# Image 0's keys and values as products of quarters, and the weight sums of p and z moved one image on

## The chip, the cores and the metric

The kernel runs on one core of a Trainium2 chip. The metric is the device time of one execution in microseconds (us). Before the change the median of three runs is 2768.2 us (2767.59 to 2768.71).

## What is computed

The input has B = 8 images of C = 512 channels and T = 32 x 32 = 1024 positions, in float32. Two attention blocks follow each other, each with a residual. The reference, cut to what matters:

```python
def _L0_conv_ref(x, ...):                       # 8 heads of 64 channels
    h = group_norm(x)                           # 32 groups
    qkv = einsum('oc,bct->bot', w_qkv, h) + b_qkv
    weight = softmax(einsum('bct,bcs->bts', q * scale, k * scale))
    a = einsum('bts,bcs->bct', weight, v)
    return x + einsum('oc,bct->bot', w_proj, a) + b_proj

def _L1_conv_ref(x, ...):                       # one head of 512 channels
    xn = group_norm(x)                          # 8 groups
    q, k, v = (conv1x1(xn, w, b) for each)
    attn = softmax(einsum('bqc,bck->bqk', q, k) * C**-0.5)
    out = einsum('bqk,bkc->bqc', attn, v)
    return x + conv1x1(out, p_w, p_b)
```

## The kernel before

**Names.** q, k, v and p are the weights of the first block (p its output projection). The second block's four weights are folded into two products of weights, made once: m (keys with queries) and z (output projection with values). A tile of 128 partitions holds 128 channels, so an image is four tiles of 128x1024. A "big" tile is one of a pool of `NBIG` equal buffers; `wpool` holds three buffers for weights.

**Products by halves.** A product of a 512x512 weight with an image is not made with eight products of halves but with seven (the Strassen-Winograd scheme). `left_sums` makes the sums of weight blocks, `right_sums` those of image blocks, and `wino` (line 229) orders the seven products over three PSUM banks a, b and c. That is "halves once". `conv` makes a product by channel (queries and keys), `by_token` (line 379) makes values, where positions lie on the partitions.

`conv2` (line 536) goes by halves twice: each of the seven products is split again into seven, so 49 products of quarters. It needs two further sets of sums:

- the inner factors of the image (`inner_factors`, line 423): 7 times 4 subtractions of 128x256 on GpSimd (POOL);
- the second sums of the weight (`keep2_steps`, line 302): after the four first sums of 128x512 on VectorE (DVE), four sums of 128x896, then seven stores to DRAM (`wdram2`). `load_weight` (line 340) brings them back, one part at a time, in the order of the list `uses` (line 333).

In `conv2`, ScalarE copies and DVE additions empty PSUM, and POOL adds a few finished blocks to others (`more`). The last two steps of each stretch are put on the list `tail` and are run by `finish` after the first product of the next stretch.

**Order of the work.** Matmuls stand in TensorE's queue in the order of the program (`keep_in_program_order`), and so do many operations of the other engines. `prologue` (line 936) does, in this order: transposes of two weights of the second block (`natural`, line 893), the product m (`product`, line 903) with the group norm of image 0 in between, then for image 0 the values, queries and keys, all by halves once; then transposes of a third weight (tr_wv), the mean of image 1's group norm, the bias products, the product z (ps_wz, 32 matmuls) and the variance of image 1's group norm. DVE makes v's second sums, POOL those of q, k, m and p. Stores and loads are issued by SyncE (SP), in order too.

**Attention of the first block.** `attention0` (line 677) goes over four pairs of heads (hp) and two halves of the queries (tb), so eight tiles, here numbered 0 to 7: tile n is hp n // 2, tb n % 2. In a tile TensorE makes scores sc (8 pieces), ScalarE their exponentials e, DVE adds the e's up in `total` (seven additions of 128x1024: one of line 698, six of line 700), and TensorE then makes av from the e's and v. After each second tile (tb = 1) `reciprocals` (line 631) has TensorE sum `total` over partitions (`sums`); these matmuls stand in TensorE's queue ahead of the next tile's sc, and wait for DVE's last addition of the tile just done. Then DVE copies `line`, SP sends it through DRAM (rows, cols, all_rows, r; DVE makes recs from cols on the way), and a tile later DVE multiplies a by r.

Other work is hung into 16 slots of this loop: slot 2n stands before av of tile n, slot 2n + 1 after it. An operation in a slot stands in its engine's queue at that place of the program. In image 0 slot 3 holds z's first sums (DVE), slots 5, 7, 9 and 11 one of z's second sums each (POOL), slot 12 their stores and two loads. Image 1's slots 4 and 5 hold mean and variance of the second block's group norm.

```python
for f in extra.pop(0) if extra else ():      # attention0: slot 2n
    f()
av = acc_tile(f"av_{uid}")
...
after = extra.pop(0) if extra else []        # slot 2n + 1
```

## Time and profile before

| What | Value |
|---|---|
| median of three runs | 2768.2 us |
| profiled execution | 2768.3 us, span 2765.8 us |
| mean granted TensorE clock | 0.999 |
| TensorE busy | 2753.6 us of the span |
| VectorE, ScalarE, GpSimd busy | 2045.6, 998.4, 1291.4 us |
| first attention of image 0 begins | 117.85 us |
| image 0: v, then q, then k | from 25.25, from 49.50, to 97.56 us |

The page gives each engine's busy time, and the chain of work that ended last, followed back from the last instruction. The view of waits lists what an engine waited for. A timeline gives an engine's instructions from the start of the span, equal neighbours in one line: start, duration of all, engine, line, operation, output<-input, shapes, count, and in brackets the idle time before with what ended it. Matmuls are pipelined, so a step's length on TensorE is read from start to start.

### The profile page before, as it was taken

What the parts mean: (1) busy time and instruction counts of PE and PEld (TensorE: products, weight loads), DVE (VectorE), ACT (ScalarE), POOL (GpSimd) and SP (SyncE); (2) the same over time, 40 slices, a digit from 0 to 9 for tenths busy, and PEclk for the clock granted to TensorE, in tenths of its full rate; (3) what the DMA queues carried; (4) which work ended last, traced back from release to release, by engine and by line L of the source; (5) the groups of instructions that cost most, each with busy time, mean ns of one, the idle gap of its engine ahead of it and who ended that gap; (6) DMA issues with size and microseconds to landing.
All of it is one profiled execution on the core that took longest, in us unless ns stands there. A gap on an engine that the chain in (4) does not pass through costs nothing.

```text
span 2765.8 us, 36809 instructions
## 1 busy us (share of the span) xinstructions
PE 2753.6 (100%) x13436; PEld 1762.1 (64%) x13436; DVE 2045.6 (74%) x3214; ACT 998.4 (36%) x1307; POOL 1291.4 (47%) x1384
## 2 busy tenths in 40 slices
PE   9999999999999999999999999999999999999999
PEld 5437736776376853868538694486844968348585
DVE  6587777777777777777777867777678776787776
ACT  1253454214632146312453125531255313633130
POOL 2313605745067440774307752176621766146763
PEclk9999999999999999999999999999999999999999
DMA  7827412344113441144401443114521145112302
GB/s 265 253 91 252 181 32 70 138 159 166 40 63 138 170 162 32 63 161 167 150 24 63 177 182 119 32 55 184 196 98 49 58 153 216 59 54 97 142 24 74
DMA packets 126070, 332.60 MB, mean 120 GB/s; under 512 B 19831, under 2 KB 64695, under 8 KB 114362
## 3 DMA queue, kind: packets, MB, share of 16 engines
q1 hardware_dynamic: 125294, 329.75, 33.6%
q8 instruction: 108, 1.77, 0.3%
q14 instruction: 80, 0.66, 0.1%
q10 hardware_dynamic: 588, 0.42, 0.1%
HBM read 258.14 MB, written 71.99 MB: 119 GB/s over the span
## 4 chain that ended last, share of the span: by engine, by line
PE 99%; DVE 1%; DMA 0%; issue 0%; SPq 0%; DVEq 0%
PE sc L60 16%; PE av L60 16%; PE psb_av L60 6%; PE psb L60 5%; PE psa_av L60 4%; PE psc_av L60 4%; PE psc L60 4%; PE psa L60 3%; PE psb_v L60 3%; PE psb_k L60 3%; PE psb_p L60 3%; PE psb_q L60 3%; PE psb_g L60 3%; PE psb_z L60 3%; PE psc_z L60 2%; PE psa_k L60 2%
## 5 line engine op out<-in xcount | busy, mean ns | idle before, releaser
L700 DVE TENSOR_TENSOR sum<-sum,e 128x1024 f32<-128x1024 f32 x384 | 473.9, 1234 | 35.5 <-ACT e L696 0.9
L696 ACT ACTIVATE e<-sc 128x1024 f32<-128x1024 f32 x512 | 476.1, 1053 | 63.1 <-PE sc L60 62.6
L60 PE MATMUL sc<-q,k 64*128 64x512 f32 x2048 | 456.8, 596 | 0.0
L60 PE MATMUL av<-e,v 128*64 128x512 f32 x2048 | 453.4, 595 | 0.0
L60 PEld LDWEIGHTS sc<-q,k 64*128 64x128 f32 x2048 | 190.1, 185 | 245.9 <-ACT e L696 120.9
L60 PEld LDWEIGHTS av<-e,v 128*64 128x64 f32 x2048 | 141.4, 137 | 299.0 <-issue 288.2
L434 POOL TENSOR_TENSOR inner_h<-x 128x256 f32<-128x256 f32 x16 | 14.8, 924 | 415.9 <-DVE x L1028 415.9
L698 DVE TENSOR_TENSOR sum<-e,e 128x1024 f32<-128x1024 f32 x64 | 79.9, 1249 | 103.6 <-ACT e L696 103.6
L719 ACT COPY a<-av 128x512 f32<-128x512 f32 x64 | 37.5, 586 | 320.1 <-PE av L60 280.6
L126 POOL TENSOR_TENSOR rstd<-ve,mhalf 128x4 f32<-128x4 f32 x16 | 18.8, 1177 | 274.0 <-DVE ve L124 274.0
L60 PE MATMUL psb<-inner,inner_h 128*128 128x256 f32 x448 | 115.6, 380 | 0.0
L60 PE MATMUL psa_av<-e,z 128*128 128x512 f32 x256 | 112.5, 592 | 0.0
L482 ACT COPY psb_v<-psa_v 128x512 f32<-128x512 f32 (+1 forms) x28 | 14.5, 517 | 232.5 <-DVE x L845 176.6
L60 PEld LDWEIGHTS psb<-inner,inner_h 128*128 128x128 f32 x448 | 84.5, 190 | 13.6 <-POOL inner L449 2.1
L60 PE MATMUL psb_z<-w_z,inner_h 128*128 128x128 f32 x672 | 87.5, 276 | 0.0
L60 PE MATMUL psb_g<-inner_h,w_m 128*128 128x256 f32 x336 | 84.9, 381 | 0.0
L776 ACT ACTIVATE e<-e 128x1024 f32<-128x1024 f32 x64 | 65.1, 1052 | 46.7 <-DVE e L766 25.6
L60 PEld LDWEIGHTS psb_z<-w_z,inner_h 128*128 128x128 f32 x672 | 81.4, 192 | 0.5
L60 PEld LDWEIGHTS psa_av<-e,z 128*128 128x128 f32 x256 | 47.4, 190 | 53.6 <-issue 51.7
L771 POOL TENSOR_TENSOR e<-e,e 128x512 f32<-128x512 f32 x64 | 79.3, 1271 | 2.0 <-DVE e L766 1.8
L571 POOL TENSOR_TENSOR v<-v,v 128x256 f32<-128x256 f32 x28 | 20.1, 726 | 125.3 <-DVE u_v L566 121.3
L820 POOL TENSOR_TENSOR t<-e,t 128x1024 f32<-128x1024 f32 x32 | 78.4, 2482 | 0.0
(443 smaller groups left out, 6138.0 us busy)
## 6 DMA issues: line engine op xcount, KB each, us to landing
r<-all_rows SPq DMA_DIRECT2D x78, 256.0 KB
x<-in_x SPq DMA_DIRECT2D x36, 512.0 KB
h<-in_x SPq DMA_DIRECT2D x32, 512.0 KB
spill<-x SPq DMA_DIRECT2D x32, 512.0 KB
x<-spill SPq DMA_DIRECT2D x32, 512.0 KB
out<-x SPq DMA_DIRECT2D x63, 256.0 KB
kept<-a SPq DMA_DIRECT2D x28, 512.0 KB
again<-kept SPq DMA_DIRECT2D x28, 512.0 KB
```

The lines of the kernel that those rows point to most:

```text
L60: tc.keep_in_program_order(nc.tensor.matmul(*args, **kw))
L126: nc.gpsimd.tensor_tensor(rstd, ve, mhalf, ALU.pow)
L434: pin(engine.tensor_tensor(dst, x, y, ALU.subtract))
L482: nc.scalar.copy(ps["b"], ps["a"])
L571: nc.gpsimd.tensor_tensor(d, x, y, ALU.add)
L696: nc.scalar.activation(e, sc, AF.Exp, scale=(C // 8) ** -0.5)
L698: nc.vector.tensor_add(total, es[0], e)
L700: nc.vector.tensor_add(total, total, e)
L719: nc.scalar.copy(dst, av)
L771: nc.gpsimd.tensor_tensor(blocks(dst, r, cc)[0], blocks(x, r, cc)[0], blocks(y, r, cc)[0], ALU.add)
L776: nc.scalar.activation(e[c, cc, r], e[c, cc, r], AF.Exp, scale=scale)
L820: on = lambda *a: lambda: tc.keep_in_program_order(nc.gpsimd.tensor_tensor(*a))
```

## The change

Of image 0, only the queries still go by halves once, and they come first. Keys and values go through `conv2`. Their second sums are made in place of the weight tile and used straight from there (`own`), with no loads. The order of the new prologue: m with the norm of image 0, q, transposes tr_wv, bias products (in bank c), three quarters of z's product, k (with z's last quarter, deferred into `tail`, behind k's first products), v. DVE makes k's second sums, POOL the inner factors and the second sums of v, q and m. `natural` copies wq in two halves. Image 1's mean and variance move into slots 0 and 1 of image 0's attention, in two halves of 64 columns.

p's sums, and the store of its first sums (`keep`, 1.8 MB), move from the prologue to the slots of image 0's attention that z's held. z's move to image 1's attention: loads at the start of that iteration, first sums in slot 5 (DVE), second sums in slots 6 and 7 (POOL), stores and two loads in slot 12; `uses` is shifted to suit.

```diff
-NBIG = 34
+NBIG = 35
...
-        def keep2_steps(n, t, engine=nc.gpsimd, pin=lambda ins: ins):
-
-            if engine is nc.gpsimd:
-                u = wpool.tile([P, 4, 7, P], F32, tag="w", name=f"prepare2_{n}")
-                u = [u[:, i, :, :] for i in range(4)]
-            else:
-                u = [big_tile(f"prepare2_{n}_{i}", (P, 7, P)) for i in range(4)]
+        def second_sums(n, t, engine, pin=lambda ins: ins, inside=True):
+
             quarter = lambda k, i: t[:, :, k, ts(i, P)]
             a11, a21, a12, a22 = quarter(0, 0), quarter(0, 1), quarter(1, 0), quarter(1, 1)
-            s1, s2, s3, s4 = u
+            if inside:
+                s3 = a21
+                s1, s2, s4 = (big_tile(f"prepare2_{n}_{i}", (P, 7, P)) for i in range(3))
+            else:
+                u = wpool.tile([P, 4, 7, P], F32, tag="w", name=f"prepare2_{n}")
+                s1, s2, s3, s4 = (u[:, i, :, :] for i in range(4))
+            f2 = (a11, a12, s4, a22, s1, s2, s3)
...
         for b in range(1, B - 1):
-            uses += [*twice["m"], *twice["z"], *layer0, *twice["p"]]
+            m0, m1 = twice["m"]
+            uses += [m0, *([None] * 2 * (b == 1)), m1, *twice["z"], *layer0, *twice["p"]]
...
+        def z_factors():
+            t, steps = prepare("z")
+            sums = second_sums("z", t, nc.gpsimd, pin, False)[1]
+            load = lambda: load_weight(pin)
+            return {5: steps, 6: sums[:2], 7: sums[2:4], 12: [sums[4], load, load]}
...
-        def natural(wt, nm, banks):
+        def natural(wt, nm, banks, cut=1):
...
-            spread(lambda o, copy: tc.keep_in_program_order(copy(t[o], pt[o])), KC)
+            for h in range(cut):
+                spread(lambda o, copy: tc.keep_in_program_order(copy(t[o][:, ts(h, C // cut)], pt[o][:, ts(h, C // cut)])), KC)
...
+            for ic in range(KC - defer):
+                part(ic)
+            if defer:
+                tail.append(lambda: part(KC - 1))
...
-            for f in first["v"][1]:
+            for f in first["q"][1]:
                 f()
-            background.extend(steps)
-            background.extend(first["q"][1])
-            v = by_token(weight_factors(first["v"][0]), hf, "v0_0", middle=(2, 5, 6, 7), back=4)
+            inner, ih = inner_factors(hf, "h0_0", tc.keep_in_program_order)
+            background.extend([*steps, *first["k"][1], ih[6], *ih[:6]])
+            q = conv(weight_factors(first["q"][0]), hf, pcols("bq0"), "q0_0", middle=(2, 5, 6, 7), back=4)
             finish()
-            run_background(len(background))
-            keep2("v", first["v"][0], nc.vector)
-            background.extend(first["k"][1])
-            x1 = [load_x(1, c, "x1") for c in range(KC)] if B > 1 else []
-            norm1 = GroupNorm(0, "0_1")
-            background.extend(lambda c=c: norm1.stats(c, x1[c]) for c in range(len(x1)))
-            q = conv(weight_factors(first["q"][0]), hf, pcols("bq0"), "q0_0")
-            keep2("q", first["q"][0])
-            keep2("k", first["k"][0])
-            t, steps = prepare("m")
-            k = conv(weight_factors(first["k"][0]), hf, pcols("bk0"), "k0_0", hooks=[[], [], [], [], steps])
-            finish()
+            all_background()
+
+            wv = natural(raw_v, "v", ("a", "acc"))
+            wk2, k_sums = second_sums("k", first["k"][0], nc.vector)
+            for f in k_sums[:4]:
+                f()
+            bias = bias_products([(wk, "bq1"), (raw_p, "bv1"), (raw_p0, "bv0")])
+            norm1, x1, made = GroupNorm(0, "0_1", halves=True), [load_x(1, c, "x1") for c in range(KC)], {}
+            for f in (k_sums[4], *first["v"][1]):
+                f()
+            for c in range(KC):
+                norm1.stats(c, x1[c])
+            product(wv, raw_p, "z", banks="bbbc", defer=True)
...
+            wv2, v_sums = second_sums("v", first["v"][0], nc.gpsimd)
+            _, q_sums = second_sums("q", first["q"][0], nc.gpsimd)
+            k = conv2(
+                "k", inner, None, "k0_0",
+                [v_sums, [*q_sums, lambda: ready("m")], [], [lambda: sum_up("m")]], own=wk2,
+            )
+            m_sums = second_sums("m", made["m"][0], nc.gpsimd)[1]
+            v = conv2(
+                "v", inner, None, "v0_0", [m_sums, [], [], []], by_tokens=True, own=wv2,
+            )
             p0, p0_steps = prepare("p")
...
+            p_sums = second_sums("p", p0, nc.gpsimd, pin, False)[1]
+            _, _, mean, affine = norm_hooks(norm1, "0_1")
             later = {
-                3: steps, 4: [load], 5: second[:1], 7: second[1:2], 9: second[2:3], 11: second[3:4], 12: [
-                    second[4], load, load,
+                0: mean, 1: affine, 3: [*p0_steps, lambda: pin(keep("p", p0))], 4: [load], 5: p_sums[:1], 7: p_sums[1:2],
+                9: p_sums[2:3], 11: p_sums[3:4], 12: [
+                    p_sums[4], load, load,
...
-            for i, fs in plan.items():
+            for i, fs in [*plan.items(), *(z_factors().items() if b == 1 else ())]:
                 extra[i] += fs
```

More of the change, by code (lines that the diff above doesn't have):

```diff
@@ L219, in run_background, with all_background @@
                 background.pop(0)()
+        def all_background():
+            run_background(len(background))
         tail = []
@@ L273, in wino @@
             tail.extend([lambda: step(4), lambda: step(3), *after])
+        pin = tc.keep_in_program_order
         wdram = {n: dram.tile([P, 7, 2, C // 2], F32, name=f"sums_{n}") for n in weights}
@@ L300, in main_path @@
         wdram2 = {n: dram.tile([P, 7, 7, P], F32, name=f"sums2_{n}") for n in "qkmvpz"}
-        def keep2_steps(n, t, engine=nc.gpsimd, pin=lambda ins: ins):
-            if engine is nc.gpsimd:
-                u = wpool.tile([P, 4, 7, P], F32, tag="w", name=f"prepare2_{n}")
-                u = [u[:, i, :, :] for i in range(4)]
-            else:
-                u = [big_tile(f"prepare2_{n}_{i}", (P, 7, P)) for i in range(4)]
+        def second_sums(n, t, engine, pin=lambda ins: ins, inside=True):
             quarter = lambda k, i: t[:, :, k, ts(i, P)]
             a11, a21, a12, a22 = quarter(0, 0), quarter(0, 1), quarter(1, 0), quarter(1, 1)
-            s1, s2, s3, s4 = u
+            if inside:
[5 more added lines that the diff above has]
+            f2 = (a11, a12, s4, a22, s1, s2, s3)
             def store():
-                for j, f in enumerate((a11, a12, s4, a22, s1, s2, s3)):
+                for j, f in enumerate(f2):
                     pin(nc.sync.dma_start(wdram2[n][:, :, j, :], f))
-            return [
+            return lambda p, j: f2[j - 1][:, ORDER.index(p), :], [
                 *(
@@ L325, in keep2_steps, with keep2 @@
             ]
-        def keep2(n, t, engine=nc.gpsimd):
-            for f in keep2_steps(n, t, engine):
+        def keep2(n, t):
+            for f in second_sums(n, t, nc.gpsimd, inside=False)[1]:
                 f()
@@ L340, in load_weight @@
         def load_weight(pin=lambda ins: ins):
-            if uses:
-                n = uses.pop(0)
+            n = uses.pop(0) if uses else None
+            if n is not None:
                 t = wpool.tile([P, 7 * C], F32, tag="w", name=f"w_{n[0]}_{len(uses)}")
@@ L377, in by_channel @@
             wino(uid, mm, done, **kw)
-        def by_token(wf, hf, name, **kw):
-            out = [big_tile(f"{name}_{j}", (P, 2, C)) for j in range(NS // 2)]
-            def mm(p, i, ps, start):
-                for jj in range(2):
-                    for k in range(2):
-                        matmul(
-                            ps[:, ts(jj, C // 2)], hf[p][k][:, ts(2 * i + jj, P)], wf[p][:, k, :],
-                            start=start and (jj, k) == (0, 0), stop=(jj, k) == (1, 1), skip_group_check=True,
-                        )
-            def done(i, r, c, ps, u):
-                dst = out[2 * c + i][:, :, ts(r, C // 2)]
-                src = ps.rearrange("p (a b) -> p a b", a=2)
-                if u is None:
-                    nc.scalar.copy(dst, src)
-                else:
-                    nc.vector.tensor_add(dst, src, u.rearrange("p (a b) -> p a b", a=2))
-            wino(name, mm, done, **kw)
-            return out
+        def z_factors():
[3 more added lines that the diff above has]
+            return {5: steps, 6: sums[:2], 7: sums[2:4], 12: [sums[4], load, load]}
         def biased(out, bias):
@@ L534, in inner_steps, with conv2 @@
             return step, run
-        def conv2(n, f, bias, name, hooks=(), after=(), by_tokens=False, alone=False):
+        def conv2(n, f, bias, name, hooks=(), after=(), by_tokens=False, alone=False, own=None):
             out = channel_tiles(name)
@@ L585, in written, with weight_of @@
                     return [(t, 2 * i + r) for t, (i, _) in zip(to, y)]
-                w = weights2[s // 2][:, (0, 2, 0, 1)[s] :]
+                def weight_of(i, j):
+                    if own:
+                        return own(products[i], j)
+                    return weights2[s // 2][:, (0, 2, 0, 1)[s] + i, j - 1, :]
                 def mm(ps, j, start):
                     for i, p in enumerate(products):
-                        wt = w[:, i, j - 1, :]
+                        wt = weight_of(i, j)
                         if not by_tokens:
@@ L613, in conv2 @@
             second = []
-            weights2 = [weight_part((n, 0))]
+            load = [] if own else [load_weight]
+            weights2 = [] if own else [weight_part((n, 0))]
             pair(0, (1, 5), [(1, 0), (1, 1)], None, [])[1]()
             pair(
-                1, (2, 6), [(0, 0), (0, 1)], [(1, 0), (1, 0)], [load_weight, lambda: biased_half(0, 0)], defer=second,
+                1, (2, 6), [(0, 0), (0, 1)], [(1, 0), (1, 0)], [*load, lambda: biased_half(0, 0)], defer=second,
             )[1]()
-            weights2.append(weight_part((n, 1)))
+            if not own:
+                weights2.append(weight_part((n, 1)))
             ahead, end = pair(
-                3, (3, 4), [(0, 1), (1, 0)], [(0, 1), (1, 0)], [load_weight, *after],
+                3, (3, 4), [(0, 1), (1, 0)], [(0, 1), (1, 0)], [*load, *after],
                 order=(-3, 6, 5, -4, 7, 2) if alone else (-3, 6, -4, 2, 5, 7),
@@ L873, in values1, with norm_hooks, by_head @@
             wino(f"av_{uid}", mm, done, middle=(2, 5, 6, 7), hooks=hooks, back=4, early=early if last else None)
+        def norm_hooks(norm, uid):
+            return [
+                [], [all_background], [lambda: norm.group_mean(acc_tile(f"gmean_{uid}")[:, :KC])],
+                [lambda: norm.affine(acc_tile(f"gvar_{uid}")[:, :KC])],
+            ]
+        def by_head(v):
+            return lambda s, head: v[head // 2][:, s * P + head % 2 * 64 : s * P + head % 2 * 64 + 64]
         def raw(n, i):
@@ L899, in natural, with product, part @@
                     transpose(pt[o][:, ts(kc, P)], wt[kc][:, ts(o, P)], ident[0])
-            spread(lambda o, copy: tc.keep_in_program_order(copy(t[o], pt[o])), KC)
+            for h in range(cut):
+                spread(lambda o, copy: tc.keep_in_program_order(copy(t[o][:, ts(h, C // cut)], pt[o][:, ts(h, C // cut)])), KC)
             return t
-        def product(lhs, rhs, nm, hooks=(), bank="a"):
+        def product(lhs, rhs, nm, hooks=(), banks="aaaa", defer=False):
             hooks = dict(hooks)
             ts_ = [pair_tile(f"prod{nm}_{h}") for h in range(2)]
-            for ic in range(KC):
-                ps = ps_tile(bank, f"ps_w{nm}_{ic}")
+            def part(ic):
+                ps = ps_tile(banks[ic], f"ps_w{nm}_{ic}")
                 for kc in range(KC):
@@ L917, in product @@
                     )
+            for ic in range(KC - defer):
+                part(ic)
+            if defer:
+                tail.append(lambda: part(KC - 1))
         def bias_products(lhs):
             n = len(lhs)
-            ps = acc_tile("ps_bias")
+            ps = ps_tile("c", "ps_bias")
             for kc in range(KC):
@@ L936, in prologue @@
         def prologue():
-            ident.append(big_tile("ident", (P, P)))
+            ident.append(rpool.tile([P, 2, 2, P], F32, tag="line", bufs=1, name="ident")[:, 0, 0, :])
             make_identity(nc, ident[0])
@@ L941, in prologue @@
             h0 = [load_x(0, c, "h0") for c in range(KC)]
-            first = {n: prepare(n) for n in "vqk"}
+            first = {n: prepare(n) for n in "qk"}
+            raw_v, raw_p0, raw_p = raw("v", 6), raw("p0", 3), raw("p", 7)
+            first["v"] = prepare("v")
             wk = natural(raw_k, "k", ("a", "b"))
-            wq = natural(raw_q, "q", ("c", "acc"))
+            wq = natural(raw_q, "q", ("c", "acc"), 2)
             norm = GroupNorm(0, "0_0", pinned=True)
@@ L957, in prologue @@
             )
-            raw_v = raw("v", 6)
-            raw_p = raw("p", 7)
-            for f in first["v"][1]:
-                f()
-            background.extend(steps)
-            background.extend(first["q"][1])
-            v = by_token(weight_factors(first["v"][0]), hf, "v0_0", middle=(2, 5, 6, 7), back=4)
+            for f in first["q"][1]:
+                f()
+            inner, ih = inner_factors(hf, "h0_0", tc.keep_in_program_order)
+            background.extend([*steps, *first["k"][1], ih[6], *ih[:6]])
@@ L973, in prologue @@
-            keep2("q", first["q"][0])
-            keep2("k", first["k"][0])
-            t, steps = prepare("m")
-            k = conv(weight_factors(first["k"][0]), hf, pcols("bk0"), "k0_0", hooks=[[], [], [], [], steps])
-            finish()
-            p0, p0_steps = prepare("p")
-            raw_p0 = raw("p0", 3)
-            keep2("m", t)
-            wv = natural(raw_v, "v", "bc")
-            norm1.group_mean(acc_tile("gmean_0_1")[:, :KC])
-            for f in p0_steps:
-                f()
@@ L985, in prologue @@
-            keep2("p", p0)
-            keep("p", p0)
-            bias = bias_products([(wk, "bq1"), (raw_p, "bv1"), (raw_p0, "bv0")])
-            product(wv, raw_p, "z", bank="b")
-            norm1.affine(acc_tile("gvar_0_1")[:, :KC])
-            t, steps = prepare("z")
-            load = lambda: load_weight(tc.keep_in_program_order)
-            second = keep2_steps("z", t, pin=tc.keep_in_program_order)
-            later = {
-                3: steps, 4: [load], 5: second[:1], 7: second[1:2], 9: second[2:3], 11: second[3:4], 12: [
-                    second[4], load, load,
-                    lambda: tc.keep_in_program_order(nc.vector.tensor_copy(ubias, bias[0])),
-                    lambda: tc.keep_in_program_order(nc.vector.tensor_add(obias[1], bias[1], pcols("bp1"))),
-                    lambda: tc.keep_in_program_order(nc.vector.tensor_add(obias[0], bias[2], pcols("bp0"))),
+            all_background()
@@ new lines, in prologue, with ready, sum_up @@
+            product(wv, raw_p, "z", banks="bbbc", defer=True)
+            def ready(n):
+                made[n] = prepare(n)
+            def sum_up(n):
+                for f in made[n][1]:
+                    f()
+            wv2, v_sums = second_sums("v", first["v"][0], nc.gpsimd)
[4 more added lines that the diff above has]
+            )
@@ new lines, in prologue @@
+            m_sums = second_sums("m", made["m"][0], nc.gpsimd)[1]
+            v = conv2(
+                "v", inner, None, "v0_0", [m_sums, [], [], []], by_tokens=True, own=wv2,
+            )
+            p0, p0_steps = prepare("p")
+            load = lambda: load_weight(pin)
+            p_sums = second_sums("p", p0, nc.gpsimd, pin, False)[1]
+            _, _, mean, affine = norm_hooks(norm1, "0_1")
+            later = {
+                0: mean, 1: affine, 3: [*p0_steps, lambda: pin(keep("p", p0))], 4: [load], 5: p_sums[:1], 7: p_sums[1:2],
+                9: p_sums[2:3], 11: p_sums[3:4], 12: [
+                    p_sums[4], load, load,
+                    lambda: pin(nc.vector.tensor_copy(ubias, bias[0])),
+                    lambda: pin(nc.vector.tensor_add(obias[1], bias[1], pcols("bp1"))),
+                    lambda: pin(nc.vector.tensor_add(obias[0], bias[2], pcols("bp0"))),
@@ L999, in prologue @@
                 ],
             }
-            return lambda s, head: v[s // 2][:, s % 2, ts(head, 64)], q, k, norm1, later
+            return by_head(v), q, k, norm1, later
         psum_pools("first", 2)
@@ L1011, in load_again @@
             return t
-        def all_background():
-            run_background(len(background))
         def begun(load, norm, b, what):
@@ L1104, in projection2 @@
             }
-        def norm_hooks(norm, uid):
-            return [
-                [], [all_background], [lambda: norm.group_mean(acc_tile(f"gmean_{uid}")[:, :KC])],
-                [lambda: norm.affine(acc_tile(f"gvar_{uid}")[:, :KC])],
-            ]
         def values(b, f, hooks=()):
@@ L1127, in values @@
             v = conv2("v", f, None, f"v0_{b}", hooks, by_tokens=True)
-            return lambda s, head: v[head // 2][:, s * P + head % 2 * 64 : s * P + head % 2 * 64 + 64], norm
+            return by_head(v), norm
         def keys_and_queries(b, f, norm, loads, factors, q_hooks):
```

## The prediction

> **What bounds the kernel now.** I read the page first (busy times, the chain that ended last), then TensorE's waits, then timelines of each engine around the places that the change touches. Page of the kernel before, sections 1 and 4:

> ```profile
> PE 2753.6 (100%) x13436; PEld 1762.1 (64%) x13436; DVE 2045.6 (74%) x3214; ACT 998.4 (36%) x1307; POOL 1291.4 (47%) x1384
> ...
> PE 99%; DVE 1%; DMA 0%; issue 0%; SPq 0%; DVEq 0%
> ```

> The view of TensorE's waits (waited for: us in total, times, longest):

> ```profile
> PE tr_wk L63 <- DMA rawk<-in_w: 3.8, 1, 3.8
> PE tr_wv L63 <- DVE k L410: 0.5, 1, 0.5
> PE ps_wm L60 <- DVE natq L900: 0.5, 1, 0.5
> PE psb_v L60 <- DVE u_v L566: 0.5, 1, 0.5
> PE tr_wq L63 <- DMA rawq<-in_w: 0.2, 1, 0.2
> PE psc_v L60 <- DVE c_v L566: 0.2, 1, 0.2
> ```

> TensorE works in a written order and waits for under 6 us of 2765.8. So two things alone move the time: matmul time taken out or put in, and new waits in TensorE's queue. Work on the other engines counts only where a matmul waits for it. TensorE's timeline of the prologue, and the starts of value and key products of image 1, which already go by halves twice:

> ```profile
> 25.25 1.97 PE L60 MATMUL psa_v<-prepare_v,h 128*128 128x256 f32 x8
> ...
> 98.57 1.64 PE L63 MATMUL tr_wv<-ident,rawv 128*128 128x128 f32 x13 [0.52 <-DVE k L410]
> 100.05 0.28 PE L60 MATMUL gmean<-mv,gm 128*128 128x4 f32 x2
> ...
> 103.80 14.00 PE L60 MATMUL ps_wz<-rawp,natv 128*128 128x512 f32 x32
> 117.64 0.28 PE L60 MATMUL gvar<-dv,gm 128*128 128x4 f32 x2
> ```
> ```profile
> 233.53 0.71 PE L60 MATMUL psa_v<-w_v,h 128*128 128x128 f32 x4
> ...
> 256.08 0.60 PE L60 MATMUL psa_k<-h,w_k 128*128 128x256 f32 x2
> ...
> 277.74 0.59 PE L60 MATMUL psa_q<-h,w_q 128*128 128x256 f32 x2
> ```

> To be seen: by starts, v of image 0 takes 49.50 - 25.25 = 24.25 us (q starts at 49.50), and q and k together 97.56 - 49.50 = 48.06, so 24.03 each. Key queries of image 1 run 277.74 to 298.89 (start of p), 21.15; v there takes 22.55, of which 0.62 are the two waits on u_v and c_v: 21.93.

> **The change part by part (prologue).** The sum stands against the profiled execution: 2768.3 us, with a span of 2765.8 and 2.5 around it. The median of the three runs is 2768.2, so it stands 0.1 above.

> 1. k of image 0, halves twice: 24.03 to 21.15, -2.88. v: 24.25 to 21.93, -2.32. q stays.
> 2. The wait of tr_wv on k (0.52) goes: tr_wv now follows q and takes banks a and acc, which q's last steps don't hold. -0.52. If acc or a is late after all it stays: bounds -0.52 and 0.
> 3. Group mean and variance of image 1 leave the prologue: 117.85 - 117.64 = 0.21 and 100.26 - 100.05 = 0.21, -0.42. They come back in slots 0 and 1 of the attention as two halves each; image 1's own gvar halves cost 365.30 - 365.14 = 0.16, so +0.32 for both.
> 4. wq's copies in halves: the first product can start about 0.3 earlier, but DVE has four pieces instead of two 0.69 copies, each with its fixed part, ahead of image 0's statistics (x4 pairs, 11.10 to 16.80). gmean comes about 0.17 later: +0.17, between -0.3 (statistics early) and +0.5.
> 5. The deferred quarter of z (14.00 / 4 = 3.5) only moves, behind k's first products.

> Sum of the prologue: -2.88 - 2.32 - 0.52 - 0.42 + 0.32 + 0.17 = -5.65; the first attention starts near 111.9 instead of 117.85.

> Costed at nothing, with cover. Inner factors (28 POOL subtractions, 0.73 each at 238.28 and up to 1.7 beside DVE): they run under q and end near 50; k needs them at 65. k's second sums (4 x 1.09 on DVE): 52 to 57, under transposes and bias products. v's and q's second sums on POOL (128x896, 2.08 alone, 2.47 contended): 61 to 70 and 70 to 78; k's own POOL additions are queued behind q's and are wanted near 82, some 4 us of cover. m's loads stand on SP behind the stores of v's and q's sums (eight of 0.45 MB; at the 285 GB/s that such stores show around 108 us they land near 84): m lands near 87. m's four first sums stand in DVE's queue ahead of k's last additions, wanted near 91. m's second sums on POOL, 94 to 102, stand ahead of v's POOL additions, wanted near 104. Each is a step of 2 to 4 us of cover; beyond it TensorE waits one for one.

> **Image 0's attention.** p's sums take exactly the places of z's: 4 DVE operations in slot 3, 4 POOL operations after them. Two timelines of before show what that does (POOL, then DVE):

> ```profile
> 146.89 10.30 POOL L318 TENSOR_TENSOR prepare_z<-prepare_z 128x896 f32<-128x896 f32 x4 [26.84 <-DVE prepare_z L292]
> ```
> ```profile
> 150.22 1.99 DVE L698 TENSOR_TENSOR sum<-e,e 128x1024 f32<-128x1024 f32 x1 [2.38 <-ACT e L696]
> 152.14 0.24 DVE L662 RECIPROCAL recs<-cols 128x16 f32<-128x16 f32 x1
> 152.32 11.28 DVE L700 TENSOR_TENSOR sum<-sum,e 128x1024 f32<-128x1024 f32 x6
> ```

> DVE additions that take 1.22 alone take 1.99, 2.92 and 2.93 while POOL works: the two alternate, about 3.03 per pair. That is harmless in tile 2, because no sums matmul follows it. New here: p's 1.8 MB store stands on SP ahead of the rows of tile 1. It takes 1.43 to issue (122.56) and some 4.6 at 400 GB/s; recs then come near 155 or 156. DVE waits for POOL's last operation until 156 anyway, so I take 0; if recs come at 158, tile 3's sums are 2 late. Bounds 0 and +2.

> **Image 1's attention, the term that decides.** z's sums move to slot 5, so they meet tile 3, which has a sums matmul behind it. DVE before:

> ```profile
> 365.42 0.16 DVE L124 TENSOR_SCALAR ve<-gvar 128x4 f32<-128x4 f32 x1 [0.37 <-PE gvar L60]
> 368.51 1.22 DVE L698 TENSOR_TENSOR sum<-e,e 128x1024 f32<-128x1024 f32 x1 [2.93 <-ACT e L696]
> 369.83 7.87 DVE L700 TENSOR_TENSOR sum<-sum,e 128x1024 f32<-128x1024 f32 x6
> 380.52 0.69 DVE L655 COPY line<-sums 128x512 f32<-128x512 f32 x1 [2.82 <-PE sums L60]
> ```
> ```profile
> 379.38 1.07 PE L60 MATMUL sums<-sum,ones 128*32 128x256 f32 x16
> ```

> In these times: the four first sums (0.69 and 1.90 at slot 3) fill the gap from 365.58 to 368.2. POOL's first second sum runs 368.3 to 370.35; the first addition, ready at 368.51, gets through by 371.4. Three more pairs of 3.03 bring the fourth addition to 380.6; three further ones at 1.33 end at 384.6. Now they end at 377.7, and TensorE is ready for sums at 379.38. So sums waits 384.65 - 379.38 = 5.2, and everything behind it in TensorE's queue too (the next sc). Nothing gives this back, since TensorE is never ahead of demand later. Bounds: 0 if POOL's operations ran at another time than DVE's additions, 6.5 if all four operations took 3.08 and blocked fully. I take +5.2, nearest to the rows of image 0.

> [...]

> Total: 2768.3 - 5.65 + 5.2 = 2767.9; I write 2768.0.

> **Rivals.** A measurement of this kernel tells about 0.2% (5.5 us) from no change, so the bounds are 2762.7 and 2773.7.
> - *The additions of tile 3 are not delayed* (POOL's sums come elsewhere, or z's wait hides): 2768.3 - 5.65 = 2762.65, just faster. For it: tile 2's contention cost TensorE nothing. Against it: tile 2 had 14 us more until its sums. Between: each microsecond less of wait is one less.
> - *Slower: m's loads hold DVE in k.* Place: m's first sums in DVE's queue ahead of k's last additions. If v's and q's second sums run contended (up to 3.08 an operation, 8 us in all), q's last store lands near 92 and m near 95, TensorE waits 4; v's POOL additions are pushed by the same amount, beyond their 2. At 97 for m the total passes 2773.7; likely value 2775. For it: in before, a POOL sum of q took 2.47 on the mean. Against: DVE's additions in k read PSUM and one SBUF tile, and such operations held 0.69 beside POOL at 64 to 81 us.
> - *The products by halves twice bring nothing* because TensorE waits for inner factors at 65: 15 us of cover, so hardly; without the 5.20 of step 1 the sum is 2773.1.

> **How the numbers follow.** Forecast (gain and wait cancel, small remainders) 0.64. Tile 3 not delayed, or by under 0.3: 0.09, all of faster. m's loads or another of the prologue's chains late by over 5.8: 0.20, and the inner factors, the clock or p's store on top of smaller waits: 0.07, together 0.27 slower. Prologue waits of 0 to 4 lie inside the forecast. The range leaves about one in ten on each side: 2762.6, the rival without the wait, and 2776, one above the slow rival. The forecast's own range is 2765 to 2773.

> **What would show it.** sc of image 0 starts near 111.9; k spans 21.15 plus 3.5 of z; v 21.9. In image 1, the waits list sums <- DVE sum with about 5 us, and tile 3's additions come 3.03 apart four times. Wrong: a wait in psb_k, psb_v or psc_v of the prologue above 2, sums without a wait, or a granted clock under 1 after it.

## The result and the profile after

The changed kernel takes 2772.77 us in the median of 22 runs (2771.0 to 2776.6), the kernel before 2768.12 us in 22 runs (2767.5 to 2768.8): ratio 1.0018, 95% interval 1.0012 to 1.0024. It is slower by 4.65 us where "no change" was forecast, inside the range. Two things are new: the loss, and a spread four times as wide. The profiled execution took 2771.6 us, with a span of 2769.8.

The view of TensorE's waits of the changed kernel (waited for: us in total, times, longest):

```profile
PE sums L60 <- DVE sum L695: 4.5, 1, 4.5
PE tr_wk L63 <- DMA rawk<-in_w: 3.7, 1, 3.7
PE psb_v L60 <- DVE v L556: 1.3, 1, 1.3
PE psc_v L60 <- DVE x L840: 0.7, 1, 0.7
PE psb_v L60 <- DVE u_v L556: 0.5, 1, 0.5
PE gmean L60 <- PE ps_wm L60: 0.4, 1, 0.4
PE ps_wm L60 <- DVE natq L906: 0.2, 1, 0.2
PE psc_v L60 <- DVE c_v L556: 0.2, 1, 0.2
```

New, of half a microsecond or more, are the wait of sums (4.5), one of psb_v (1.3) and one of psc_v (0.7). TensorE's timeline, prologue and then tile 3 of image 1:

```profile
25.26 7.10 PE L60 MATMUL psa_q<-h,prepare_q 128*128 128x512 f32 x16
...
49.37 1.91 PE L63 MATMUL tr_wv<-ident,rawv 128*128 128x128 f32 x16
...
97.48 2.05 PE L60 MATMUL psb_v<-prepare_v,inner_h 128*128 128x128 f32 x16 [1.32 <-DVE v L556]
...
113.52 7.43 PE L60 MATMUL sc<-q,k 64*128 64x512 f32 x32
```
```profile
375.70 0.64 PE L60 MATMUL sums<-sum,ones 128*32 128x256 f32 x8
380.83 1.08 PE L60 MATMUL sums<-sum,ones 128*32 128x256 f32 x8 [4.49 <-DVE sum L695]
381.84 8.31 PE L60 MATMUL sc<-q,k 64*128 64x512 f32 x32
390.08 7.09 PE L60 MATMUL av<-e,v 128*64 128x512 f32 x32
```

The first attention starts at 113.52 instead of 117.85. In tile 3 of image 1 half of the sums matmuls run at once, the other half 4.49 us late; the scores after them take 8.31 us where other tiles' take about 7.1. DVE and POOL there:

```profile
361.81 0.68 DVE L296 TENSOR_TENSOR prepare_z<-prepare_z 128x512 f32<-128x512 f32 x1
362.53 1.90 DVE L297 TENSOR_TENSOR prepare_z<-prepare_z 128x512 f32<-128x512 f32 x3
364.77 1.23 DVE L693 TENSOR_TENSOR sum<-e,e 128x1024 f32<-128x1024 f32 x1 [0.35 <-ACT e L691]
366.10 14.68 DVE L695 TENSOR_TENSOR sum<-sum,e 128x1024 f32<-128x1024 f32 x6
```
```profile
364.81 12.23 POOL L325 TENSOR_TENSOR prepare_z<-prepare_z 128x896 f32<-128x896 f32 x4
```

Six additions take 14.68 us instead of 7.87, beside four POOL operations; one by one, the first five of them start 3.03 us apart, as the prediction had it. Why the scores are slow is seen in the table by stretches (us, then busy us with count of PE, PEld, DVE, ACT, POOL, then the granted clock of TensorE, DMA share, GB/s):

```profile
377.42:380.83 3.41, 0.00 (x0) 0.00 (x0) 3.15 (x3) 0.00 (x0) 0.00 (x0) 1.00 0.00 0
380.83:384.24 3.41, 3.41 (x14) 1.39 (x16) 0.69 (x1) 0.27 (x1) 0.00 (x0) 0.50 0.03 7
384.24:387.66 3.42, 3.42 (x18) 1.52 (x16) 1.55 (x3) 3.36 (x4) 0.00 (x0) 1.00 0.02 2
```

For 3.41 us after the wait TensorE has half its clock.

Where the time went, by comparing the start of the same matmul in both traces (after less before):

| At | Difference, us | Step |
|---|---|---|
| first scores of image 0 | -4.32 | prologue |
| second tile of image 0 | -3.85 | +0.47: halves of the mean, and 0.3 more in tile 0's scores, gone in runs 5 and 7 |
| first scores of image 1 | -3.68 | +0.17 |
| late sums of tile 3 | +0.99 | +4.67, of it 4.49 the wait |
| behind the slow scores of the next tile | +2.63 | +1.64: half clock |
| last matmul | +4.22 | +1.59, of it 0.73 a wait of psc_v in image 3 |

### The profile page after: what moved, and what is told of

The parts are those of the page before. It is cut to its first block, busy times and chain, and to the rows that moved or that the text cites. A ratio compares the mean times of both kernels' runs of the same rounds, so it can differ in the third digit from the quotient of the medians.

```text
span 2769.8 us, 37196 instructions
## 1 busy us (share of the span) xinstructions
PE 2751.9 (99%) x13566; PEld 1772.6 (64%) x13566; DVE 2058.5 (74%) x3256; ACT 1002.6 (36%) x1317; POOL 1330.6 (48%) x1428
## 3 DMA queue, kind: packets, MB, share of 16 engines
q8 instruction: 109, 1.79, 0.3%
## 4 chain that ended last, share of the span: by engine, by line
PE 95%; DVE 3%; DMA 1%; POOL 0%; issue 0%; SPq 0%; ACT 0%; DVEq 0%; POOLq 0%
PE sc L60 16%; PE av L60 15%; PE psb_av L60 5%; PE psb L60 5%; PE psa_av L60 4%; PE psc_av L60 4%; PE psc L60 4%; PE psa L60 3%; PE psb_q L60 3%; PE psb_p L60 3%; PE psb_g L60 3%; PE psb_z L60 3%; PE psb_v L60 3%; PE psb_k L60 2%; PE psc_z L60 2%; PE psa_g L60 2%
## 5 line engine op out<-in xcount | busy, mean ns | idle before, releaser
L695 DVE TENSOR_TENSOR sum<-sum,e 128x1024 f32<-128x1024 f32 x384 | 480.7, 1252 | 36.1 <-DVE mv L96 0.7
L60 PE MATMUL sc<-q,k 64*128 64x512 f32 x2048 | 458.5, 597 | 0.0
L60 PE MATMUL av<-e,v 128*64 128x512 f32 x2048 | 453.4, 595 | 0.0
L60 PEld LDWEIGHTS sc<-q,k 64*128 64x128 f32 x2048 | 191.1, 186 | 246.4 <-ACT e L691 115.5
L60 PEld LDWEIGHTS av<-e,v 128*64 128x64 f32 x2048 | 141.4, 137 | 298.3 <-issue 278.4
L60 PE MATMUL psb<-inner,inner_h 128*128 128x256 f32 x448 | 115.6, 380 | 0.0
L60 PE MATMUL psa_av<-e,z 128*128 128x512 f32 x256 | 112.5, 592 | 0.0
L60 PEld LDWEIGHTS psb<-inner,inner_h 128*128 128x128 f32 x448 | 84.5, 190 | 13.6 <-POOL inner L439 2.1
L60 PE MATMUL psb_z<-w_z,inner_h 128*128 128x128 f32 x672 | 87.5, 276 | 0.0
L60 PE MATMUL psb_g<-inner_h,w_m 128*128 128x256 f32 x336 | 84.9, 381 | 0.0
L60 PEld LDWEIGHTS psb_z<-w_z,inner_h 128*128 128x128 f32 x672 | 81.4, 192 | 0.5
L60 PEld LDWEIGHTS psa_av<-e,z 128*128 128x128 f32 x256 | 47.4, 190 | 53.6 <-issue 51.7
L561 POOL TENSOR_TENSOR k<-k,k 128x256 f32<-128x256 f32 x32 | 25.1, 795 | 112.2 <-DVE u_k L556 109.1
```

Of the source, the lines that this page charges most:

```text
L60: tc.keep_in_program_order(nc.tensor.matmul(*args, **kw))
L561: nc.gpsimd.tensor_tensor(d, x, y, ALU.add)
L695: nc.vector.tensor_add(total, total, e)
```

## The experiments

All are edits of the changed kernel. Each was timed beside the kernel before on the same chip; its median was 2768.25 us for the first four runs and 2768.34 for the last three.

**1. z's sums one tile later.**

```diff
-            return {5: steps, 6: sums[:2], 7: sums[2:4], 12: [sums[4], load, load]}
+            return {7: steps, 8: sums[:2], 9: sums[2:4], 12: [sums[4], load, load]}
```

> z's first sums in slot 7 and its second sums in slots 8 and 9 of image 1, so beside tile 4, which has no sums matmul behind it; nothing else differs from the changed kernel. Theory (tile 3's additions are held by GpSimd's sums, TensorE idles 4.5 us, its clock then drops and costs 1.6 more in some executions): no wait of sums, granted clock 1.00 behind it, time 2772.8 - 4.5 - 0.5 to 1.6 = 2766.7 to 2767.8, and the executions lie as close together as those of before (1.4 us from end to end). Rival (the loss after tile 3 is only moved): the same wait at tile 5's sums, time near 2772.8. Rival for the clock (the slow stretch behind tile 3 has nothing to do with the wait): 2768.3 and still a stretch of about 0.6 of the clock.

Measured: 2766.84 us (2765.8 to 2769.4; ratio 0.9995, 0.9986 to 1.0004). TensorE's timeline in tile 3:

```profile
375.60 1.07 PE L60 MATMUL sums<-sum,ones 128*32 128x256 f32 x16
376.60 1.98 PE L60 MATMUL sc<-q,k 64*128 64x512 f32 x7
```

All 16 matmuls run without a wait, and the clock stays at 1.00 (each microsecond from 374 to 386). Some backlog reaches tile 5, whose sums wait 0.79. So, by the medians, 5.9 us were owed to the place of z's sums: the wait and the slow stretch went together. The spread, 3.6 us, did not close as expected; runs 6 and 7 point to the wait of psb_v.

**2. z's second sums on VectorE, in the old place.**

```diff
-            sums = second_sums("z", t, nc.gpsimd, pin, False)[1]
+            sums = second_sums("z", t, nc.vector, pin, False)[1]
...
-            return {5: steps, 6: sums[:2], 7: sums[2:4], 12: [sums[4], load, load]}
+            return {5: [*steps, *sums[:4]], 12: [sums[4], load, load]}
```

> z's four second sums are made by VectorE in slot 5, right behind the first sums, instead of by GpSimd: no operation of GpSimd beside tile 3's additions, but 4 x 1.09 = 4.4 us more in VectorE's queue. [...] Time 2772.8 - 2.8 - 0.5 to 1.6 = 2768.4 to 2769.5. Rival (the wait is not from contention but from the amount of work): wait of 4 us or more, 2772.8.

Measured: 2768.66 us (2767.6 to 2771.7; ratio 1.0001, 0.9992 to 1.0010). DVE, then TensorE:

```profile
365.10 4.22 DVE L325 TENSOR_TENSOR prepare_z<-prepare_z 128x896 f32<-128x896 f32 x4
369.24 1.22 DVE L693 TENSOR_TENSOR sum<-e,e 128x1024 f32<-128x1024 f32 x1
370.56 7.87 DVE L695 TENSOR_TENSOR sum<-sum,e 128x1024 f32<-128x1024 f32 x6
```
```profile
376.34 0.64 PE L60 MATMUL sums<-sum,ones 128*32 128x256 f32 x8
378.48 0.64 PE L60 MATMUL sums<-sum,ones 128*32 128x256 f32 x8 [1.50 <-DVE sum L695]
```

The same four sums cost VectorE 4.22 us when it makes them itself, and some 7 when POOL makes them beside it (14.68 - 7.87 = 6.8). The wait falls from 4.5 to 1.5, where the expected time counts 2.8 less, and no clock drop follows it (1.00 in each microsecond from 375 to 390). A second wait of 0.9 appears at a later sums.

**3. The wait from VectorE's own work.** First sums in slot 5, then nine additions whose output is overwritten; second sums in slots 8 and 9.

```diff
+            u = second_tiles[-1]
+            dose = lambda: pin(nc.vector.tensor_tensor(u[:, 0], t[:, :, 0, ts(1, P)], t[:, :, 1, ts(1, P)], ALU.add))
-            return {7: steps, 8: sums[:2], 9: sums[2:4], 12: [sums[4], load, load]}
+            return {5: [*steps, *[dose] * 9], 8: sums[:2], 9: sums[2:4], 12: [sums[4], load, load]}
```

> z's sums as in the run with slots 7 to 9, but first sums in slot 5 and nine additions of 128x896 on VectorE behind them that serve nothing (their output is overwritten): about 9.8 us more in VectorE's queue ahead of tile 3's additions, with no work of GpSimd. The wait should be 1.09 x 9 - 2.7 = 7.1 us. [...] Rival (the drop is owed to GpSimd's work or to chance): clock 1.00 behind the wait, 2773.8.

Measured: 2772.90 us (2771.8 to 2775.2; ratio 1.0017, 1.0008 to 1.0026). The dose was smaller than meant: the extra additions came to stand between tile 3's own, the last behind them, and the wait was 4.35 us instead of 7.1. In size it is the wait of the changed kernel without POOL's work beside it, and the clock drops here too. The profiled execution shows two drops, one already in the prologue (same columns as above):

```profile
96.19:99.60 3.41, 1.33 (x13) 1.14 (x12) 3.41 (x7) 0.57 (x1) 0.54 (x1) 1.00 0.80 272
99.60:103.02 3.42, 3.42 (x16) 3.42 (x17) 0.53 (x1) 0.58 (x1) 3.34 (x2) 0.50 0.78 237
103.02:106.43 3.41, 3.41 (x32) 3.41 (x32) 2.72 (x7) 0.00 (x0) 3.41 (x3) 1.00 0.53 166
...
382.91:386.32 3.41, 1.88 (x10) 0.71 (x12) 3.17 (x4) 0.00 (x0) 0.80 (x1) 0.50 0.02 5
386.32:389.74 3.42, 3.42 (x10) 1.36 (x8) 0.00 (x0) 1.48 (x2) 3.34 (x3) 0.50 0.03 5
```

The first follows the wait of psb_v, 2.08 us long in this execution: in the 3.41 us ahead of the drop TensorE was busy for 1.33. So POOL is not needed for a drop, and a wait of 2.08 can be enough. In the traces all six waits above 2 us (behind the first 10 us) are met by a drop; only one execution of each kernel has a trace, so for the others it is not shown.

**4. m's sums later, in v.**

```diff
-                [v_sums, [*q_sums, lambda: ready("m")], [], [lambda: sum_up("m")]], own=wk2,
+                [v_sums, [*q_sums, lambda: ready("m")], [], []], own=wk2,
...
-                "v", inner, None, "v0_0", [m_sums, [], [], []], by_tokens=True, own=wv2,
+                "v", inner, None, "v0_0", [[], [lambda: sum_up("m"), *m_sums], [], []], by_tokens=True, own=wv2,
```

> m's first sums move from k's last hook to v's second hook, its second sums behind them; the rest is the changed kernel. Theory (VectorE stands at m's first sums until m's loads land at 93.9 us, and v's additions behind it hold TensorE 1.3 us): the wait of psb_v goes, scores of image 0 start 1.3 earlier, time 2772.8 - 1.3 = 2771.5. Rival (the four first sums themselves, 2.9 us in VectorE's queue, hold v's additions wherever they stand): the wait moves to another psb_v or psc_v of v and the time stays within 0.5 of 2772.8.

Measured: 2780.68 us (5 runs, 2779.3 to 2781.5; ratio 1.0043, 1.0029 to 1.0057). Both expectations missed the time. The wait of psb_v is gone and one of psc_v has come, as the rival had it, but far longer and by another cause: POOL now makes m's second sums ahead of v's own additions at a worse time, and VectorE stands for those (POOL, VectorE, then TensorE):

```profile
112.72 2.07 POOL L325 TENSOR_TENSOR prepare_m<-prepare_m,prepare_m 128x896 f32<-128x896 f32 x1
114.74 1.41 POOL L561 TENSOR_TENSOR v<-v,v 128x256 f32<-128x256 f32 x2
```
```profile
116.18 0.42 DVE L556 TENSOR_TENSOR v<-psa_v,v 128x256 f32<-128x256 f32 x1 [6.15 <-POOL v L561]
```
```profile
118.69 1.22 PE L60 MATMUL psc_v<-prepare_v,h 128*128 128x128 f32 x4 [6.75 <-DVE c_v L556]
```

A price that the prediction named, "v's POOL additions are pushed", is 6.75 us here, with a clock drop that begins in it. The 1.3 us itself is real, and this is not the way to remove it.

**5. q's second sums ahead of v's**, so that q's buffer comes free earlier and m's loads can go into it.

```diff
-            wv2, v_sums = second_sums("v", first["v"][0], nc.gpsimd)
             _, q_sums = second_sums("q", first["q"][0], nc.gpsimd)
+            wv2, v_sums = second_sums("v", first["v"][0], nc.gpsimd)
...
-                [v_sums, [*q_sums, lambda: ready("m")], [], [lambda: sum_up("m")]], own=wk2,
+                [[*q_sums, lambda: ready("m")], v_sums, [], [lambda: sum_up("m")]], own=wk2,
```

> The changed kernel with q's second sums ahead of v's on GpSimd, and m's loads on SyncE behind q's stores, ahead of v's last three stores. m's loads wait until q's last store has landed, because they go into q's buffer. Theory: they land near 85 us instead of 93.9, VectorE makes m's first sums as soon as it comes to them (near 91), and the wait of psb_v (1.3 us in the profile of the changed kernel, 2.1 with a drop of the clock behind it in the run with nine extra additions) is gone: 2772.8 - 1.3 to 3 = 2769.8 to 2771.5. Rival (GpSimd is what holds v): v's second sums end near 78 instead of 69.5, v needs them at 88, no new wait; if the old one stays, 2772.8.

Measured: 2770.95 us (2769.1 to 2772.2; ratio 1.0008, 0.9999 to 1.0017). SP's wait (from the view of waits, 60 to 125 us), its queue and then DVE, first of the changed kernel:

```profile
SPq L291 <- DMA sums_q<-prepare_q: 4.4, 1, 4.4
```
```profile
88.44 1.91 SPq L291 DMA_DIRECT2D prepare_m<-product_m  x4
```
```profile
93.99 0.69 DVE L296 TENSOR_TENSOR prepare_m<-prepare_m 128x512 f32<-128x512 f32 x1 [2.67 <-DMA prepare_m<-product_m]
```

and of this run:

```profile
83.90 1.91 SPq L291 DMA_DIRECT2D prepare_m<-product_m  x4
```
```profile
89.63 0.69 DVE L296 TENSOR_TENSOR prepare_m<-prepare_m 128x512 f32<-128x512 f32 x1
```

m's loads are issued 4.5 us earlier, VectorE no longer stands for them, and psb_v's wait of 1.3 is gone; v gets its second sums from POOL 10 us later and does not wait. The 4.5 us of sums stay, and in this execution they are followed by two slow stretches instead of one:

```profile
375.21:378.62 3.41, 0.00 (x0) 0.00 (x0) 3.20 (x3) 0.00 (x0) 0.50 (x1) 1.00 0.00 0
378.62:382.03 3.41, 2.53 (x12) 1.05 (x14) 1.52 (x2) 0.00 (x0) 0.00 (x0) 0.50 0.03 5
382.03:385.45 3.42, 3.42 (x10) 1.36 (x8) 0.05 (x1) 2.05 (x2) 0.00 (x0) 0.50 0.03 5
```

The wait is as long as in the changed kernel (4.50 and 4.49), the slow work after it 6.83 us less the idle part instead of 3.41: against the changed kernel the lead shrinks from 1.34 us at the scores of tile 3 (360.28 against 361.62) to 0.07 after the slow scores (397.03 against 397.10), so the drop cost 1.64 + 1.27 = 2.9 us.

**6. All of z's sums on VectorE in slot 7.** Edit as in 2, with 7 in place of 5.

> z's first and second sums all on VectorE in slot 7, beside tile 4; the rest is the changed kernel. With GpSimd making the second sums there, tile 4's backlog still cost 0.8 us at tile 5's sums. On VectorE they take 4.4 us of its own instead of holding it for some 7: the backlog is gone by tile 5's sums, no wait of sums at all, time 2766.8 - 0.8 = 2766.0. Rival (contention costs no more than doing the work on VectorE): wait of 0.8 stays, 2766.8.

Measured: 2767.96 us (2765.0 to 2770.1; ratio 0.9998, 0.9989 to 1.0007), 2 us over the expectation. The waits of sums shrink to 0.9 in two, of it 0.2 at tile 5. Part of what is over it lies in the prologue, which this run leaves alone: the first scores start 0.8 later than in run 1, where psb_v waits 1.29; here it waits 1.96 (1.32 in the changed kernel, 2.08 in run 3). Another part is the second wait of sums, 0.7 at 2464 us: it shows in the three runs with z's sums on VectorE (0.88 in run 2, 0.46 in run 7) and in no other, and why stays open. Executions differ by up to 5 us.

**7. Edits 5 and 6 together.**

> Both edits together: q's second sums first, and z's sums on VectorE in slot 7. If the two losses are separate, the gains add: 2766.0 - 1.3 = 2764.7, which is the gain of the prologue with hardly anything given back (2768.2 - 5.65 would be 2762.6), and faster than the kernel before by 3.5 us. If one loss takes the place of the other, it stays near 2766.

Measured: 2764.76 us (2763.6 to 2765.4; ratio to the kernel before 0.9986, 0.9977 to 0.9995). The losses are separate, and this version is faster than both kernels, by 3.6 us than the one before. Its waits:

```profile
PE tr_wk L63 <- DMA rawk<-in_w: 4.3, 2, 3.8
PE sums L60 <- DVE sum L695: 0.7, 2, 0.5
PE psc_v L60 <- DVE x L840: 0.5, 1, 0.5
PE psb_v L60 <- DVE u_v L556: 0.5, 1, 0.5
...
```

No half clock is recorded from 10 us on until the last 5 us (mean clock 1.000), and with the long waits most of the spread is gone too: 1.8 us (11 runs), against 5.6 (22 runs) in the changed kernel.

## Why the prediction was wrong

**What held.** Products by halves twice gave nearly what the rows of image 1 said: added up over their own matmuls in run 7, where m's loads are mended, k takes 21.15 us as forecast and v 22.19 instead of 21.93. For v there was luck in it: the 22.55 us read for image 1 count 1.00 of sums that image 0 doesn't have, and leave out v's last 1.79, which stand behind psa_k. In run 7 the first scores start 5.07 us earlier; -5.65 less the 0.32 that comes back later, so -5.97, was forecast. Of the 0.9 between them 0.85 lies ahead of the first product of q (26.10 us against v's 25.25 before); over the traces of the changed kernel and its variants that start lies anywhere from 25.21 to 26.62. The half copies of wq cost nothing (gmean at 16.90 in both). Image 0's tile 2 is slow as z's was, its sums at 171.34 wait for nothing, and p's store delayed recs to 151.38, which is 155.2 on the time scale of the kernel before (3.85 us later), where "155 or 156" was forecast. The decisive term, the wait in tile 3, was put in its place and by its mechanism: 5.2 forecast, 4.49 measured, with four pairs 3.03 us apart. The 0.7 between them is mainly the half of the sums matmuls that runs without waiting.

**What failed.** First, the clock. The forecast has no term for it, only a place among the causes of the 0.07, and no row of before tells what a clock drop behind such a wait costs; a granted clock under 1 is named as a sign of being wrong. The clock does drop behind the wait; it cost 1.64 us in the profiled execution, and 2.9 in run 5. A row of before had been misread: 16 transposes tr_wk stand behind 3.83 us of idling, at a clock of 1.00, and were taken to run at full speed (timeline, then table by stretches):

```profile
3.83 3.58 PE L63 MATMUL tr_wk<-ident,rawk 128*128 128x128 f32 x16 [3.83 <-DMA rawk<-in_w]
```
```profile
3.80:7.00 3.20, 3.17 (x14) 2.57 (x15) 0.00 (x0) 0.00 (x0) 0.00 (x0) 1.00 1.06 361
```

The timeline of the changed kernel shows the opposite:

```profile
3.73 3.91 PE L63 MATMUL tr_wk<-ident,rawk 128*128 128x128 f32 x16 [3.73 <-DMA rawk<-in_w]
7.44 2.62 PE L63 MATMUL tr_wq<-ident,rawq 128*128 128x128 f32 x16
```

The first 16 transposes take 3.7 us from start to start, the next 16 take 2.6, and the 16 of tr_wv at 49.37 take 1.84. The lines of before had it too: 3.58 us for 16, but 1.64 for 13 of tr_wv. And the clock column is filled with 1.00 where the trace holds no record: its records of full clock begin only at 6.90 us before and 8.78 us after. Up to these times the transposes start 0.21 us apart, from then on 0.11. The evidence for full speed was an empty field.

Second, m's loads: "m lands near 87" with "2 to 4 us of cover". VectorE stood until 94.0, and TensorE paid 1.32 (1.96 and 2.08 in other executions). The loads were issued at 88.44, because they wait 4.4 us for q's last stores to land, issued at 77.9 to 83.9. The wrong number is the landing of these stores, "near 84": DMA moved some 285 GB/s, as reckoned, but until 88.1, for earlier stores and z's product stood in the queue ahead of the eight stores counted. That m's first sums hold VectorE in k was named in the slow rival, and came; its cause there, sums that run contended on POOL, did not (2.08 us each). In run 3 the wait drew a clock drop too.

Third, 1.59 us come late in the kernel, where nothing was changed. Of it 0.73 is a wait of psc_v in image 3 on a VectorE queue that stood 0.96 us for a load of the image ahead. It shows in seven of the eight traces of the changed kernel and its variants, as 0.5 to 0.9, not in run 3 and not in the kernel before. Why stays open; the rest comes in small steps, among them 0.3 in image 4 and 0.2 in image 6, not traced further.

**The sum.** Forecast -5.65 + 5.2. In the profile: -3.68 + 4.67 + 1.64 + 1.59 = 4.22 at the last matmul. So the gain was some 2 us too large, the wait half a microsecond too long, and 3.2 us stood in no term. The median lies 1.2 us above the profiled execution, as would follow if others paid more for the clock; only the mean clock of each run, given to three digits, speaks for it: of the eleven slowest runs ten show 0.998, of the eleven fastest nine show 0.999.

**The rivals.** The one without a wait in tile 3 did not happen. The third, products that bring nothing, did not either. That a measurement tells only 5.5 us from no change was too wide: with 22 runs of each kernel the interval, 1.0012 to 1.0024, leaves no change out at 4.65 us.

## What to carry to other kernels

Where one engine's queue is full and in order, price a wait with what follows it: each of the six stalls above 2 us in these traces (behind the first 10 us) met half clock, which cost a further 1.6 and 2.9 us where it was worked out. Work that fills another engine's gaps is free only in a stretch with no deadline close behind it: four such sums cost nothing beside tile 2, 0.8 us beside tile 4, and 4.5 us beside tile 3. And when a view shows a clock of 1.00, look whether the field is measured or filled in: here the records begin at 6.90 and 8.78 us.

## What the runs showed of the hardware

```
changed kernel:        0.5 from 380.83 to 384.24
run 3:                 0.5 from  99.60 to 103.02, and from 382.91 to 389.74
run 4:                 0.5 from 116.68 to 123.51, and from 389.75 to 393.16
run 5:                 0.5 from 378.62 to 385.45
```

The traces of both kernels also end at half clock, the one of before from its last 4.36 us on, the changed kernel's from its last 3.08. Each slow stretch ahead of that lasts 3.41 or 6.83 us, and within a run the starts lie whole steps apart: 283.31 us is 83 x 3.413 in run 3, 273.07 us is 80 x 3.413 in run 4.

The window just ahead of a drop, one step of the grid, need not be idle. Counted from the first record of full clock, the windows just ahead of the six drops hold 0.00 (four of them), 0.59 and 1.33 us of matmul work (the last two in run 3); one that was followed by full clock holds 2.08 (run 4, from 109.86). Run 4 shows both, a busy window of 2.08 with full clock after it and an idle one with half clock after it, and the slow one that ends with full clock (columns as above):

```profile
109.86:113.27 3.41, 2.08 (x19) 1.89 (x17) 0.18 (x1) 0.00 (x0) 3.41 (x3) 1.00 0.57 175
113.27:116.68 3.41, 0.00 (x0) 0.00 (x0) 0.42 (x1) 0.00 (x0) 3.41 (x4) 1.00 0.19 58
...
389.75:393.16 3.41, 3.09 (x14) 1.26 (x16) 0.96 (x2) 0.00 (x0) 0.00 (x0) 0.50 0.02 5
```

Not every window with work in it brings the clock back: slow ones with 1.40 (run 4), 1.88 (run 3) and 2.53 us (run 5) were followed by another slow one, those with 3.09 (run 4) and more by full clock. Where the limits lie between these figures is not shown. So the same wait of 4.5 us cost 1.64 us in the changed kernel, where it ended with a window (at 380.83), and 2.9 in run 5, where it ended 0.88 us into one (at 379.50). After run 6's wait of 1.96 us no drop came: the 16 matmuls of psb_v behind it take 1.89 us from start to start, as long as at full clock in the changed kernel (1.88). Behind run 3's wait of 2.08 us the same 16 take 3.52, at half clock.

Four sums of 128x896 on POOL held six additions of VectorE up by 6.8 us in all; the same four on VectorE took 4.22.
